# Splitting the causal mask of the scores between VectorE and ScalarE, with the places of the work set anew

## The chip, the core and the metric

The kernel runs on one core of one Trainium2 chip. The core has five engines that each work through an instruction queue of their own, in order: TensorE (matmuls), VectorE, ScalarE, GpSimd and SyncE, which here only issues DMAs. They meet at semaphores. The metric is the time of one execution on the device in microseconds (us), the median of several runs.

## What is computed

One transformer layer in fp32 for 8 sequences of 256 tokens, width 256: a layer norm, then an attention and a feed-forward part (FFN) that both read the normed input and are both added to the input.

```python
xn = layernorm(x)                                   # [8, 256, 256]
# attention, 16 heads of 128, 64 memory slots
q, k = rope(xn @ Wq.T), rope(xn @ Wk.T);  v = xn @ Wv.T;  g = xn @ Wg.T
s   = clip(xn @ Ws1.T @ Ws2.T + bs2, -32, 32)       # [b, h, t, 64]
es, enz = exp(s), exp(-cumlogsumexp(s, over tokens))
A   = where(causal, q @ k.T / sqrt(128), 0)         # scores, 256 x 256 a head and sequence
ok  = enz * (A @ es)                                # logits over the 64 slots
qv  = softmax(ok)
o   = where(causal, (qv * enz) @ es.T, 0) @ v
x1  = (rmsnorm(o) * w * silu(g)) @ Wo.T
# FFN, 2048 wide, weights as 4-bit codes with a scale for each 32
x2  = (gelu(xn @ Wg4.T) * (xn @ Wu4.T)) @ Wd4.T
out = x + x1 + x2
```

The line that matters here is `A`. The mask is causal: of a 256 x 256 block of scores, cut into four squares of 128, one lies wholly in the forbidden half and is never computed, two lie on the diagonal and need the triangle, and one, between queries 128 to 255 and keys 0 to 127, is wholly allowed.

## The kernel before

**Tiling.** The 2048 tokens are 4 groups of 512 (two sequences each). The attention works in 32 steps n: group g = n // 8 and a pair of heads. In each step, for the two heads j = 0, 1: `rope` (line 632) makes q and k on TensorE and turns them on ScalarE (copies of the two halves into z), VectorE (times the cosine) and GpSimd (times the sine, and the sum); `states` (575) makes es and enz; `value` and `gate` (669, 682) make v and the gate; `scores` (720), `logits` (735), `softmax` (771), `cross` (811), `weights` (835), `outputs` (879) and `close` (929) do the rest. Five kinds of data that need their rows and columns exchanged go out to DRAM and back (`scattered`, `turned`).

**The scores.** For a head j and each of the two sequences b, two matmuls fill 384 columns of one PSUM bank (of 8): keys 0 to 127 against all 256 queries (columns 0 to 255), keys 128 to 255 against queries 128 to 255 (columns 256 to 383). So the first and the third square of 128 lie on the diagonal, the second is the free one. `masked` then makes `at` in SBUF: one VectorE multiply of 384 columns with a mask whose squares are triangle, ones, triangle (`mask`, of which `tri` is the first square). `logits` multiplies `at` with es on TensorE, so it must wait for the four `at` of its step.

**The order.** The order of instructions on every engine is fixed when the program is built, by a planner written into the kernel. It holds a clock for each engine. A piece of work that follows a matmul is a generator (a "chain") whose `yield` gives the engine and a cost: `V(n)` is VectorE with 0.15 + 0.00105 n, `S(n)` ScalarE with 0.15 + 0.00088 n. `advance` always emits the instruction that could begin first; at equal times a chain of rank 0 (the masks are such) goes first. The matmuls of a step are placed by the tables: `POS` gives each unit's place in a step as a share of it, `START` other places for the steps -1 and 0 (-1 is what runs ahead of step 0), `NORM_AT` those of the later groups' norms, and `DUE` says how many pieces of FFN weights are to be decoded by each step. The FFN is cut into units (gate, up, down) that `feed` lays evenly between; `FIRST` and `LAST` weigh how many of them the first and last steps get. A unit whose operands would by the planner's clock come later than 0.3 (`SOON`) after TensorE's is put off: an FFN unit goes first, up to 4 ahead (`AHEAD`). The 8 PSUM banks go round in order, so a matmul that opens a bank waits until the reader of the bank 8 back is done.

The scores were made and masked like this:

Of the kernel before, what the change touches and what calls it, by code (L numbers as in the profile page):

```python
# [13 lines left out]
ALU = mybir.AluOpType  # L14
# [3 lines left out]
P = 128  # L18
# [14 lines left out]
WARM = 15  # L33


POS = {'scores': (0.054, 0.064),
 'logits': (0.12,),
 'softmax': (0.335,),
 'cross': (0.147,),
 'weights': (0.169,),  # L40
 'low': (0.121,),
 'states': (0.167,),
 'outputs': (0.364, 0.453),
 'close': (0.384, 0.559),
 'rope': (0.176, 0.315, 0.368, 0.485),
 'vg': (0.561, 0.79, 0.922, 0.953)}
START = {-1: {'states': (0.575,), 'rope': (0.155, 0.358, 0.421, 0.588)},
 0: {'vg': (0, 0.013, 0.059, 0.197),
     'scores': (0.082, 0.162),
     'states': (0.336,),  # L50
     'logits': (0.251,),
     'softmax': (0.433,),
     'rope': (0.211, 0.24, 0.245, 0.458)}}
FEED = {-1: (0.336, 1.0)}
NORMS = {0: 1, 2: 2, 5: 3}
WO = (1, 3, 4, 6)
NORM_AT = (0.204, 0.657)
FIRST = [0.27, 1.57]
LAST = [1.65, 3.53]
DUE = [4, 6, 7, 7, 9, 9, 10, 11, 11, 11, 12, 13, 14, 15, 16, 16, 16, 17, 18, 19, 19, 22, 23, 23, 24]  # L60


@with_exitstack
def layer_kernel(ctx: ExitStack, tc: tile.TileContext, a: dict, out: bass.AP):
# [15 lines left out]
    nc = tc.nc  # L80
# [21 lines left out]
    def V(n):  # L102
        return "v", 0.15 + 0.00105 * n

    def S(n):
        return "s", 0.15 + 0.00088 * n
# [97 lines left out]
    def bank():  # L204
        while not freed:
            advance()
        clock["pe"] = max(clock["pe"], freed.pop(0))
        t = ps_p.tile([P, 512], F32, tag="ps", name="ps", bufs=8)
        at_tag[id(t)] = t, []
        banks_taken.add(id(t))  # L210
        return t
# [6 lines left out]
    mask = const.tile([P, 3 * P], F32, tag="mask", name="mask")  # L218
    tri, ones = mask[:, 0:P], mask[:, P : 2 * P]
# [278 lines left out]
    def ffn():  # L498

        for q in range(4):  # L500
            for g in range(NG):
                for n in blocks(q):
                    yield ffn_gate, g, n
                    yield ffn_up, g, n
                for i in (0, 2):
                    yield ffn_down, g, q, i
# [204 lines left out]
        return pst, ps  # L711

    def masked(ts, pss):
        for t, ps in zip(ts, pss):
            yield V(384)
            nc.vector.tensor_tensor(t, ps[:, 0 : 3 * P], mask, ALU.mult)

    def scores(n, j):

        (q, qc), (k, kc) = of[n]["q", j], of[n]["k", j]  # L720
        need(qc, kc)
        pss, ats = [], []
        for b in range(2):
            ps = bank()
            nc.tensor.matmul(  # L725
                ps[:, 0:T], lhsT=k[:, b, 0:P], rhs=q[:, b, :], start=True, stop=True
            )
            nc.tensor.matmul(  # L728
                ps[:, T : T + P], lhsT=k[:, b, P:T], rhs=q[:, b, P:T], start=True, stop=True
            )  # L730
            pss.append(ps)
            ats.append(new(p2, [P, 3 * P], "at", 4))
        pe(1.3)
        of[n]["at", j] = ats, chain(masked(ats, pss), *ats, *pss, rank=0)
# [236 lines left out]
    banks = NG * (MLP // P * 2 + 8)  # L971
    weight = FIRST + [1.0] * (N + 2 - len(FIRST) - len(LAST)) + LAST
    feeding = list(ffn())
# [18 lines left out]
    ps = bank()  # L992
# [10 lines left out]
    for n in range(-1, N + 1):  # L1003
        at = []
        pos = START.get(n, {})

        def put(name, k, f, *args):
            place = pos.get(name, POS[name])
            at.append((place[k], len(at), f, args))

        def put_at(place, f, *args):
            at.append((place, len(at), f, args))

        def put_norm(g, places):
            for k, h in enumerate((0, 2)):
                put_at(places[k], norm, g, h)
# [24 lines left out]
        if gn:  # L1041
            if gn > 1:
                put_at(0.0, load_x, gn * TC, TC)
            put_norm(gn, NORM_AT)
        if n > 0:
# [14 lines left out]
        fed = upto  # L1060
        upto = DUE[n + 1] if n + 1 < len(DUE) else 24
        for k in range(sent, upto):
# [93 lines left out]
```

## Time and profile before

| | |
|---|---|
| median of 3 runs | 1188.27 us (1187.34 to 1188.94) |
| the profiled execution | 1187.13 us, of which the profile's span is 1185.3 us |
| instructions | 18158 |
| granted TensorE clock | 1.00 in every stretch |
| DMA | 135.30 MB, mean 114 GB/s, 38.5% of the 16 engines' time |
| HBM | read 88.47 MB, written 45.61 MB |

How the busy time lies over the span (us of busy time in each stretch; the stretches are in us from the span's start):

| stretch | TensorE | VectorE | ScalarE | GpSimd |
|---|---|---|---|---|
| 0 to 66 | 58.87 | 54.60 | 27.91 | 29.61 |
| 66 to 130 | 62.39 | 55.11 | 33.90 | 33.48 |
| 130 to 330 | 199.67 | 155.49 | 96.01 | 90.76 |
| 330 to 530 | 200.00 | 152.04 | 91.85 | 83.78 |
| 530 to 730 | 199.60 | 148.41 | 89.06 | 82.67 |
| 730 to 930 | 199.48 | 153.94 | 96.06 | 87.62 |
| 930 to 1130 | 200.00 | 139.90 | 89.80 | 79.12 |
| 1130 to 1185.3 | 51.89 | 25.20 | 11.68 | 7.07 |

In the profile a row of a group of instructions has the line of the kernel, the engine, the operation, the tiles written and read, partitions x elements, the number of instructions, then busy time in us, the mean of one in ns, and the engine's idle time just before with what ended it. TensorE's fp32 matmuls appear as two records each. A row of the timeline has start and duration in us, and in brackets an idle time before it and its releaser. Durations of neighbours overlap a little[...]. TensorE's ends are modelled, so that its busy time is not its peak rate; its waits are what can be read from it.

### The profile page before, as it was taken

The page shows a single profiled execution, that of the slowest core. Times are in us where ns is not written, and L with a number is a line of the kernel's source. Part 1 is how long each engine was busy: PE and PEld are TensorE (multiplying, and loading weights), DVE is VectorE, ACT ScalarE, POOL GpSimd, SP SyncE. Part 2 cuts the span into 40 slices and gives each one's busy share as a digit, 9 for nine tenths or more (in the row PEclk, how much of TensorE's full clock was granted, in tenths as well). Part 3 has the DMA queues.
Part 4 walks back from the last instruction along what each step waited for, and adds up shares of the span by engine and source line. Part 5 has one row for each costly group of instructions (what it writes and reads, how often), then busy time and mean ns, then how long its engine had stood idle before and what let it go on. Part 6 is the DMA issues. An engine that isn't in the chain of part 4 may idle for free.

```text
span 1185.3 us, 18158 instructions
## 1 busy us (share of the span) xinstructions
PE 1171.9 (99%) x5830; PEld 827.7 (70%) x5830; DVE 884.7 (75%) x1690; ACT 536.3 (45%) x1685; POOL 494.1 (42%) x439
## 2 busy tenths in 40 slices
PE   9899999999999999999999999999999999999998
PEld 6466776866767777667767677686776777766775
DVE  7978968887677788767587875968778577768553
ACT  3545535455344444443354543435544444445321
POOL 5434525554344444434344442434544334445110
PEclk9999999999999999999999999999999999999999
DMA  6335444453333342333344243434333333432321
GB/s 209 116 105 153 143 118 152 132 144 116 101 119 117 110 140 84 107 113 107 90 142 123 86 121 107 120 103 122 96 97 96 116 116 107 124 102 88 98 64 61
DMA packets 143087, 135.30 MB, mean 114 GB/s; under 512 B 21264, under 2 KB 110480, under 8 KB 142992
## 3 DMA queue, kind: packets, MB, share of 16 engines
q1 hardware_dynamic: 142992, 134.15, 38.5%
q8 instruction: 46, 0.75, 0.3%
q14 instruction: 49, 0.40, 0.1%
HBM read 88.47 MB, written 45.61 MB: 113 GB/s over the span
## 4 chain that ended last, share of the span: by engine, by line
PE 89%; DVE 6%; DMA 2%; issue 1%; POOL 1%; ACT 1%; SPq 1%; DVEq 0%; ACTq 0%; POOLq 0%
PE ps L645 17%; PE ps L706 17%; PE ps L491 9%; PE ps L941 9%; PE ps L437 8%; PE ps L466 8%; PE ps L888 5%; PE ps L725 4%; PE ps L745 3%; PE ps L845 3%; PE ps L728 2%; PE ps L584 2%; PE ps L872 1%; PE ps L820 1%; DVE enz L630 1%
## 5 line engine op out<-in xcount | busy, mean ns | idle before, releaser
L663 POOL TENSOR_TENSOR z<-z,turns 128x512 f32<-128x512 f32 x128 | 169.4, 1324 | 209.3 <-ACT z L656 209.0
L645 PE MATMUL ps<-xT,wts 128*128 128x512 f32 x512 | 239.2, 599 | 0.5 <-ACT xT L349 0.5
L706 PE MATMUL ps<-wts,xT 128*128 128x256 f32 x1024 | 235.7, 379 | 1.5 <-DVE og L914 1.1
L706 PEld LDWEIGHTS ps<-wts,xT 128*128 128x128 f32 x1024 | 194.4, 190 | 54.1 <-issue 24.4
L645 PEld LDWEIGHTS ps<-xT,wts 128*128 128x128 f32 x512 | 90.1, 190 | 82.0 <-issue 75.1
L446 POOL TENSOR_SCALAR t<-t 128x512 f32<-128x512 f32 x64 | 40.2, 629 | 196.6 <-ACT t L444 194.6
L437 PE MATMUL ps<-xT,w_gate 128*128 128x512 f32 x256 | 120.7, 594 | 0.1
L466 PE MATMUL ps<-xT,w_up 128*128 128x512 f32 x256 | 120.6, 594 | 0.0
L630 DVE RECIPROCAL enz<-enz 128x128 f32<-128x128 f32 x128 | 117.6, 932 | 0.0
L491 PE MATMUL ps<-w_down,inter 128*128 128x256 f32 x512 | 115.3, 380 | 0.0
L941 PE MATMUL ps<-w_o,ogT 128*128 128x256 f32 x496 | 112.1, 379 | 0.0
L941 PEld LDWEIGHTS ps<-w_o,ogT 128*128 128x128 f32 x496 | 94.1, 190 | 24.7 <-issue 12.4
L491 PEld LDWEIGHTS ps<-w_down,inter 128*128 128x128 f32 x512 | 96.6, 190 | 15.9 <-issue 3.2
L655 ACT COPY z<-ps 64x512 f32<-64x512 f32 x128 | 74.5, 582 | 69.8 <-PE ps L645 60.3
L444 ACT ACTIVATE t<-ps 128x512 f32<-128x512 f32 x64 | 38.2, 596 | 137.9 <-PE ps L437 137.8
L910 POOL TENSOR_TENSOR ss<-ss,nhalf 128x4 f32<-128x4 f32 x64 | 66.0, 1032 | 69.7 <-DVE ss L906 68.4
L409 DVE TENSOR_TENSOR res<-ps,res 128x512 f32<-128x512 f32 x63 | 42.9, 681 | 69.5 <-PE ps L491 48.0
L664 POOL TENSOR_TENSOR k<-k,z 128x512 f32<-128x512 f32 x64 | 83.7, 1308 | 26.5 <-DVE k L658 16.7
L664 POOL TENSOR_TENSOR q<-q,z 128x512 f32<-128x512 f32 x64 | 85.0, 1328 | 21.2 <-DVE q L658 17.2
L803 POOL TENSOR_TENSOR prT<-okT,enz 128x512 f32<-128x512 f32 x32 | 40.8, 1274 | 119.9 <-DMA okT<-by_way 106.6
L792 ACT ACTIVATE ok<-okT,mx 128x64 f32<-128x64 f32 x256 | 85.7, 339 | 10.8 <-DVE mx L786 10.3
L448 DVE TENSOR_TENSOR t<-ps,t 128x512 f32<-128x512 f32 x64 | 43.7, 684 | 60.9 <-POOL t L446 60.7
(83 smaller groups left out, 1936.6 us busy)
## 6 DMA issues: line engine op xcount, KB each, us to landing
wts<-in_wqkvg_dram SPq DMA_DIRECT2D x64, 512.0 KB, 3.8
by_way<-ok SPq DMA_DIRECT2D x256, 64.0 KB, 1.8
okT<-by_way SPq DMA_DIRECT2D x64, 256.0 KB, 2.7
by_way<-og SPq DMA_DIRECT2D x256, 64.0 KB, 1.8
ogT<-by_way SPq DMA_DIRECT2D x64, 256.0 KB, 2.9
by_way<-u SPq DMA_DIRECT2D x128, 64.0 KB, 1.8
u<-by_way SPq DMA_DIRECT2D x32, 256.0 KB, 2.8
pk<-in_codes_dram SPq DMA_DIRECT2D x12, 256.0 KB, 3.1
```

The lines of the kernel that those rows point to most:

```text
L437: nc.tensor.matmul(pg, lhsT=w_gate[:, c, ns], rhs=xT[:, c, gs], start=c == 0, stop=c == 1)
L466: nc.tensor.matmul(pu, lhsT=w_up[:, c, ns], rhs=xT[:, c, gs], start=c == 0, stop=c == 1)
L491: nc.tensor.matmul(ps[:, k, :], lhsT=inter[g, n][0][:, (i + k) * P : (i + k + 1) * P], rhs=w_dn[:, n, :], start=n == 2 * q, stop=n == 2 * ...
L630: nc.vector.reciprocal(r, r)
L645: nc.tensor.matmul(ps, lhsT=w[:, c, :], rhs=xT[:, c, g * G : (g + 1) * G], start=c == 0, stop=c == 1)
L655: nc.scalar.copy(z[0:64], pv[64:128])
L663: nc.gpsimd.tensor_tensor(z, z, sin_b, ALU.mult)
L664: nc.gpsimd.tensor_tensor(y, y, z, ALU.add)
L706: nc.tensor.matmul(ps[:, k, :], lhsT=xT[:, c, tt], rhs=w[:, which, c, :], start=c == 0, stop=c == 1,)
L792: nc.scalar.activation(pr[:, js, i, :], okT[:, js, i, :], AF.Exp, bias=mx[:, k : k + 1], scale=SCALE, accum_out=sm[:, k : k + 1],)
L910: nc.gpsimd.tensor_tensor(ss, ss, nhalf, ALU.pow)
L941: nc.tensor.matmul(ps[:, k, :], lhsT=ogT[hh][0][:, i + k], rhs=w_o[:, (hp // 2) * 4 + hh, :], start=hh == 0, stop=hh == 3,)
```

## The change

`masked` is rewritten. For each `at`, VectorE multiplies only the first and the third square (one instruction over 2 x 128 columns with a step between them, against the triangle used twice), and ScalarE copies the second square. Both write the same `at` tile and read the same PSUM bank. The rest of the code is as it was, with the third square of `mask` still made at the start. The tables have new numbers: the scores' place goes from 0.054 and 0.064 to 0, the logits' from 0.12 to 0.148, the softmax's, outputs', close's and low rank's are moved, so are places of the steps -1 and 0 and of the norm, the FFN's weights in the first and last steps, and four entries of `DUE`. With them the planner orders the instructions of all engines anew from the first step on; lines behind `masked` have numbers larger by 7 in the changed kernel (the multiply is L718, the copy L723).

```diff
-POS = {'scores': (0.054, 0.064),
- 'logits': (0.12,),
- 'softmax': (0.335,),
+POS = {'scores': (0, 0),
+ 'logits': (0.148,),
+ 'softmax': (0.404,),
  'cross': (0.147,),
  'weights': (0.169,),
- 'low': (0.121,),
+ 'low': (0.14,),
  'states': (0.167,),
- 'outputs': (0.364, 0.453),
- 'close': (0.384, 0.559),
+ 'outputs': (0.315, 0.453),
+ 'close': (0.367, 0.534),
...
-START = {-1: {'states': (0.575,), 'rope': (0.155, 0.358, 0.421, 0.588)},
- 0: {'vg': (0, 0.013, 0.059, 0.197),
-     'scores': (0.082, 0.162),
+START = {-1: {'states': (0.727,), 'rope': (0.155, 0.358, 0.421, 0.588)},
+ 0: {'vg': (0.044, 0.057, 0.103, 0.241),
+     'scores': (0.068, 0.162),
...
-     'softmax': (0.433,),
-     'rope': (0.211, 0.24, 0.245, 0.458)}}
+     'softmax': (0.411,),
+     'rope': (0.238, 0.267, 0.272, 0.485)}}
...
-NORM_AT = (0.204, 0.657)
-FIRST = [0.27, 1.57]
-LAST = [1.65, 3.53]
-DUE = [4, 6, 7, 7, 9, 9, 10, 11, 11, 11, 12, 13, 14, 15, 16, 16, 16, 17, 18, 19, 19, 22, 23, 23, 24]
+NORM_AT = (0.204, 0.593)
+FIRST = [0.1, 1.57]
+LAST = [1.56, 3.5]
+DUE = [4, 6, 7, 7, 8, 9, 10, 11, 11, 11, 12, 13, 14, 15, 15, 16, 16, 16, 18, 19, 19, 22, 22, 23, 24]
...
     def masked(ts, pss):
+
+        tri_b = tri.unsqueeze(1).to_broadcast([P, 2, P])
         for t, ps in zip(ts, pss):
-            yield V(384)
-            nc.vector.tensor_tensor(t, ps[:, 0 : 3 * P], mask, ALU.mult)
+            yield V(256)
+            nc.vector.tensor_tensor(
+                t.rearrange("p (k q) -> p k q", q=P)[:, ::2],
+                ps[:, 0 : 3 * P].rearrange("p (k q) -> p k q", q=P)[:, ::2], tri_b, ALU.mult,
+            )
+            yield S(128)
+            nc.scalar.copy(t[:, P : 2 * P], ps[:, P : 2 * P])
```

## The prediction

> **What bounds the kernel now.** I read the page's first part, then TensorE's waits, then the rows of the changed operation, then the timeline around it. First part (busy us, share of the span, instructions):
>
> ```profile
> PE 1171.9 (99%) x5830; PEld 827.7 (70%) x5830; DVE 884.7 (75%) x1690; ACT 536.3 (45%) x1685; POOL 494.1 (42%) x439
> ```
>
> TensorE is busy for 1171.9 of 1185.3 us, at a granted clock of 1.00 in every stretch. VectorE, which the change relieves, is busy for three quarters. All that a change beside TensorE can win is in TensorE's waits (total us, times, longest):
>
> ```profile
> PE ps L725 <- POOL k L664: 3.0, 2, 2.6
> PE ps L745 <- DVE at L716: 1.7, 3, 1.3
> PE ps L706 <- DVE og L914: 1.1, 1, 1.1
> ...
> PE ps L706 <- DVE inter L475: 0.5, 1, 0.5
> ...
> PE ps L725 <- DVE t L452: 0.4, 1, 0.4
> PE ps L745 <- DVE off L306: 0.4, 1, 0.4
> PE ps L888 <- DVE wt L855: 0.3, 1, 0.3
> ```
>
> The rest of the 13.4 us: 2.0 us before and around the first matmuls, about 3.1 us after the last one, and gaps too small for a name, the same in both kernels. What can change is 7.0 us. By the timeline, step by step: n=0 0.40+0.48, n=1 2.61+1.34+0.19, n=3 1.06+0.40, later 0.18+0.38. (The 0.33 at 1145.7 us stays: the last 19 groups of TensorE's program are the same.) Even all of it would be 0.6%. The line that the change rewrites, with its neighbours by size, from the groups with shapes kept apart (busy us, mean ns | idle before):
>
> ```profile
> L716 DVE TENSOR_TENSOR at<-ps,mask 128x384 f32<-128x384 f32 x128 | 64.1, 545 | 0.6 <-PE ps L728 0.5
> L855 DVE TENSOR_TENSOR wt<-ps,mask 128x512 f32<-128x512 f32 x64 | 40.7, 676 | 2.5 <-PE ps L845 2.5
> L598 DVE TENSOR_SCALAR esT<-ps 128x256 f32<-128x256 f32 x64 | 24.0, 416 | 19.5 <-PE ps L845 18.7
> L829 ACT COPY cross<-ps 128x256 f32<-128x256 f32 x32 | 11.9, 373 | 68.4 <-PE ps L820 68.3
> ```
>
> Only 1.7 us of TensorE's waits is put down to those 64.1 us of VectorE, in three places. A usual step shows why (start, duration; TensorE, then VectorE):
>
> ```profile
> 932.51 0.38 PE L728 MATMUL ps<-q,k 128*128 128x128 f32 x2
> 932.73 1.88 PE L437 MATMUL ps<-xT,w_gate 128*128 128x512 f32 x4
> 934.45 1.88 PE L466 MATMUL ps<-xT,w_up 128*128 128x512 f32 x4
> 936.26 1.52 PE L745 MATMUL ps<-at,es 128*64 128x256 f32 x16
> ```
> ```profile
> 931.55 1.94 DVE L716 TENSOR_TENSOR at<-ps,mask 128x384 f32<-128x384 f32 x4
> ```
>
> The scores end at 932.9, the four masks at 933.5, and the logits start at 936.26 behind two FFN units: 2.8 us to spare.
>
> **The change, part by part.**
>
> *The split.* Removed: 128 multiplies of 384 elements, 545 ns each. Added: 128 multiplies of 2x128 and 128 copies of 128. From 545 and 676 ns the slope is 1.02 ns an element, so 256 elements are about 0.41 us (L598, another operation of that size, has 416 ns); the copy, from 373 ns at 256 and 580 at 512 (L679), about 0.27 us. VectorE loses 128 x 0.13 = 17 us, ScalarE gains 128 x 0.27 = 35 us (45% to 48% busy). Neither bounds the end: directly nothing for TensorE.
>
> *The new wait.* In the built program every copy waits for VectorE, and the logits then wait for ScalarE. So the two parts of one mask are in series: 0.41 + 0.27, plus about 0.05 us of handover (VectorE to ScalarE 0.03 to 0.05 in the timeline), 0.74 us against 0.545. **Here a rule speaks against the change**: the Trainium skill, "PSUM — Partial Sum Buffer", section "Terms", says that two engines may not read one bank in the same partitions at once. By the row alone, with the copy beside the multiply, a mask would be ready 0.13 us sooner; by the rule it is 0.2 us later. No run here shows such a double read; the built program's waits side with the rule, and I take 0.2 us later. A second rule, "Perfetto Trace Analysis", section "Optimizing Scalar/DVE Operations", has each instruction pay a fixed access cost (about 125 ns for VectorE on PSUM, 51 for ScalarE) and advises grouping. By rows the fixed part of VectorE is 545 - 384 x 1.02 = 153 ns. If the split's extra engine time (0.41 + 0.27 - 0.545 = 0.14 us, 128 times) were on TensorE's path, the sum would be +18 us; by the waits only the steps without cover pay.
>
> Behind a waiting copy on ScalarE stand the tanh of the FFN gate, the copies of the next cross state and the rope's halves, on which TensorE waits through banks and operands. In the usual step they come after all four copies or are done before.
>
> *The places.* TensorE's program has the same matmuls in another order. Between the second head's scores and the logits stood 1.7 to 8.6 us of other work, mostly FFN, in 28 steps and nothing in 4 (n = 1, 3, 6, 15). Now it is the cross matmul (0.54 us) and mostly one FFN unit: at least 2.3 us in 29 steps, and 0.54 us in n = 1, 3, 31. Cover of 2.3 us against a last mask that needs 0.74 after its matmul, for a logits half that starts 0.65 us later still: 2.2 us spare, against at most one instruction ahead on each queue (0.93 VectorE, 0.60 ScalarE). Hidden. Changes of array shape cost 0.10 us each (two L491 units take 6.9 us, and 7.01 when the next is L745); there are 118, before 116: **+0.2**. DMAs: same transfers, each issued with the work that feeds it; the order on SP changes by a place or two (a turn of ok or og before or after a weight load). At 38.5% DMA share I cost that at nothing; where a turn slips behind a 512 KB load (3.8 us to landing) it hits the early steps, below.
>
> *Step 0*: now scores come before most of the value and gate work, 5 us sooner, and only 5.2 us of other work stands before the logits (8.6 before). VectorE's queue of decoding is what is late, because it stalls beside GpSimd:
>
> ```profile
> 21.69 1.42 DVE L392 TENSOR_SCALAR u<-u 128x512 int32<-128x512 int32 x1
> ```
> ```profile
> 21.18 1.65 POOL L664 TENSOR_TENSOR q<-q,z 128x512 f32<-128x512 f32 x1
> ```
>
> L392 takes 0.42 us elsewhere (36.04 us); here it ends 0.28 us after GpSimd's L664. Walking the new order with these durations: the bank of the last rope comes free at about 25.1 us, wanted at 24.4 (0.7; without the stalls 0; I take 0.35). The third and fourth mask stand behind 2 scans, 3 reciprocals, 2 FFN steps and a norm's statistics (1.27 us), and are whole at 34.0 and 35.7; the logits' halves want them at 33.3 and 34.65: 0.7 + 1.05. **2.1** (0 to 2.5), before 0.88.
>
> *Step 1*: the 2.61 us was the last rope of the step: its product came from GpSimd at 55.95, its scores were due at 53.4. Now an FFN unit (1.72) stands between the two heads' scores; the same chain (z buffer, ScalarE, two GpSimd passes of 1.27) behind a softmax pass of 1.3 us on ScalarE comes at about 55.2, due at 54.0: 1.2. Then the logits: the fourth copy stands behind the cross copy (0.37) and a tanh (0.63): 0.8. **2.0** (0.4 to 4.1), before 4.14.
>
> *Step 3*: two norm passes (1.15) and the cross copy stand before the third copy: 0.95; of the bank wait (1.06, before) I keep half: **1.45** (0.4 to 2.5), before 1.46. *Later*: in step 31 the cross copy is ahead of the last two mask copies with 0.54 us of cover: 0.6; other small waits 0.5: **1.1**, before 0.56.
>
> Sum: 2.1 + 2.0 + 1.45 + 1.1 + 0.2 = 6.85 against 7.04: -0.2 us. From the profiled execution (1185.3 us span, 1.83 around it, 1187.13) that is 1186.9; the median of the three runs shown is 1.1 above that execution, so **1188.1**.
>
> **Rivals.**
> - *The early steps run clear.* For: the split takes 0.13 us from VectorE per mask just where its queue is the late one (83% busy in the first 66 us), and the new order puts cover at both of step 1's waits. Against: step 0 loses 3.4 us of cover. Step 0 0.7, step 1 0.8, step 3 0.6, later 0.5, shapes 0.2: 2.8 us, so 1188.27 - 4.24 = 1184.0.
> - *The copies wait in every step.* Place: ScalarE's queue before the logits. With two instructions of each engine ahead of the last mask (2 x 0.68 + 2 x 0.60 + 0.74 = 3.3 us) the cover of 2.3 + 0.65 falls short by about 0.3 us; in 23 steps that is +7, 1195. It decides from 2.2 us of queue on. For: L745 waits for two engines in turn, with less cover than before. Against: in the usual step both queues stand empty there (VectorE waits 1.0 us just before 930.95).
> - *The early steps get worse*, by banks held until the copy: +4, 1192.
> - *The split does nothing that TensorE sees*: this is the first case, since only the order then counts.
>
> **How the numbers follow.** A measurement of this kernel tells about 0.2% (2.4 us) from no change. Near the old time (own range 1185.9 to 1190.6): 0.47. Early steps clear: 0.30. Copies wait everywhere 0.12, early steps worse 0.11. So faster 0.30, same 0.47, slower 0.23. The range takes in the clear case and half of the slower ones: 1183.8 to 1191.6.
>
> **What would show it.** L718 near 0.41 us and L723 near 0.27; VectorE about 17 us less, ScalarE 35 more; TensorE's busy time the same within 1 us, its waits still nearly all before 130 us, now put down to ScalarE's at in L752. Wrong if L752 waits for at in more than some five steps, or if L732's wait for k and the first logits' wait are both gone.

## The result and the profile after

The changed kernel takes 1190.72 us (median of 9 runs, 1190.15 to 1191.87) against 1187.69 for the kernel before: 1.0024 of it, 95% interval 1.0015 to 1.0032. It is slower by 3.0 us: inside the range of the forecast, but the other way from its likeliest case, a gain of 0.2 us.

First part of the page of the changed kernel (busy us, share of the span, instructions):

```profile
PE 1174.8 (99%) x5830; PEld 830.0 (70%) x5830; DVE 877.2 (74%) x1690; ACT 569.2 (48%) x1813; POOL 491.2 (41%) x439
```

The span is 1188.4 us, 3.1 more. TensorE has the same 5830 records and is "busy" 2.9 us longer: not all of the loss is waiting. The rows of the split, from the groups with shapes kept apart (busy us, mean ns | idle before):

```profile
L718 DVE TENSOR_TENSOR at<-ps,mask 128x256 f32<-128x256 f32 x128 | 50.2, 415 | 4.4 <-PE ps L735 3.9
L723 ACT COPY at<-ps 128x128 f32<-128x128 f32 x128 | 33.8, 265 | 54.1 <-DVE at L718 49.1
```

The two take 415 and 265 ns, as worked out; the copies' idle time is put down to their own multiplies. TensorE's waits (total us, times, longest):

```profile
PE ps L852 <- POOL prT L810: 4.6, 3, 3.7
PE ps L732 <- POOL k L664: 2.0, 1, 2.0
PE ps L752 <- ACT at L723: 1.1, 3, 0.7
PE ps L1001 <- DVE mask L262: 1.0, 1, 1.0
PE ps L437 <- DVE sgate L694: 0.5, 1, 0.5
```

A line stands on top that the kernel before did not have: the `weights` matmuls (L852) wait for prT, the softmax of the step before, once for 3.7 us. The logits wait for ScalarE's `at` for 1.1 us in all, in three places. The timeline of TensorE there (start, duration, and idle time before with its releaser):

```profile
61.65 0.70 PE L584 MATMUL ps<-rT,w_s 64*128 64x256 f32 x4
66.07 1.66 PE L852 MATMUL ps<-prT,esT 64*128 64x128 f32 x16 [3.72 <-POOL prT L810]
67.51 1.07 PE L879 MATMUL ps<-cross,prT 64*128 64x128 f32 x8
```

The kernel before, same place (there `weights` is L845):

```profile
61.79 3.72 PE L491 MATMUL ps<-w_down,inter 128*128 128x256 f32 x16
65.44 0.70 PE L584 MATMUL ps<-rT,w_s 64*128 64x256 f32 x4
66.07 3.72 PE L491 MATMUL ps<-w_down,inter 128*128 128x256 f32 x16
69.72 0.49 PE L845 MATMUL ps<-prT,esT 64*128 64x128 f32 x4
```

prT is not late by itself. GpSimd makes it once a step; the first of the 32 starts at 64.8 us in the changed kernel and at 67.2 before (shortest, median and longest in ns, then the first and last start):

```profile
L810 POOL TENSOR_TENSOR prT<-okT,enz x32: 1261/1271/1278, 64.8 to 1139.4; 128x512 f32<-128x512 f32 x32
L803 POOL TENSOR_TENSOR prT<-okT,enz x32: 1262/1270/1386, 67.2 to 1135.5; 128x512 f32<-128x512 f32 x32
```

But two down units, 6.9 us, stood around the states and ahead of the weights, and in the new order they stand behind the weights, so TensorE arrives at 62.3.

The other part of the loss is in how long the same matmuls take: L852's sixteen records took 1.06 us in a usual step and 1.66 here. The busy time by stretch (length, then busy us of PE, PEld, DVE, ACT and POOL; granted TensorE clock; DMA share; GB/s) of the changed kernel:

```profile
56.00:60.00 4.00, 4.00 (x20) 3.33 (x22) 4.00 (x9) 2.33 (x7) 0.62 (x1) 0.57 0.28 75
```
```profile
66.00:70.00 4.00, 3.93 (x26) 3.06 (x27) 2.20 (x5) 1.26 (x2) 0.02 (x1) 0.57 0.02 5
```

and of the kernel before, which waits 2.61 us just ahead:

```profile
57.00:60.00 3.00, 1.66 (x13) 0.99 (x12) 2.96 (x8) 0.97 (x2) 0.00 (x0) 1.00 0.35 94
```

Asked in stretches of half a microsecond, the clock of the changed kernel is 0.50 from about 56.3 to 59.7 and from about 66.6 to 70.0 us: twice 3.4 us, each right behind a wait (1.97 us for k, 3.72 for prT). At half clock a busy TensorE loses 1.7 us in such a period.

So the first theory, the **order theory**, says that the new places put TensorE idle twice in step 1, and that each time half clock follows. Its rival, the **split theory**, says that the masks are whole later and the logits pay.

### The profile page after: what moved, and what is told of

It reads as the page before. It is cut to its first block, busy times and chain, and to the rows that moved or that the text cites. A ratio compares the mean times of both kernels' runs of the same rounds, so it can differ in the third digit from the quotient of the medians.

```text
span 1188.4 us, 18234 instructions
## 1 busy us (share of the span) xinstructions
PE 1174.8 (99%) x5830; PEld 830.0 (70%) x5830; DVE 877.2 (74%) x1690; ACT 569.2 (48%) x1813; POOL 491.2 (41%) x439
## 4 chain that ended last, share of the span: by engine, by line
PE 89%; DVE 6%; DMA 2%; SPq 1%; issue 1%; ACT 1%; POOL 0%; DVEq 0%; POOLq 0%
PE ps L706 17%; PE ps L645 17%; PE ps L948 9%; PE ps L491 9%; PE ps L437 8%; PE ps L466 8%; PE ps L895 5%; PE ps L732 4%; PE ps L752 3%; PE ps L852 3%; PE ps L735 2%; PE ps L584 1%; PE ps L827 1%; PE ps L879 1%; DVE enz L630 1%
## 5 line engine op out<-in xcount | busy, mean ns | idle before, releaser
L692 ACT ACTIVATE sgate<-ps 128x512 f32<-128x512 f32 x64 | 37.9, 598 | 103.3 <-PE ps L706 97.5
L895 PEld LDWEIGHTS ps<-v,wt 128*128 128x128 f32 x512 | 67.0, 191 | 28.9 <-issue 23.0
```

The costliest lines, as they stand in the source:

```text
L895: nc.tensor.matmul(po[:, i, :], lhsT=wt[:, i, :], rhs=v[:, i, j * DK : (j + 1) * DK], start=False, stop=i == TC - 1,)
```

## Experiments

Each was timed over several rounds beside the kernel before on the same chip, which took 1187.97 us beside the first four, 1188.08 beside the next and 1187.45 beside the last. So compare the ratios, which are to it; that of the changed kernel is the 1.0024 above, as it was not timed again. The clock is the granted one, a mean over each run: one period of 3.4 us at half clock brings it to 0.9986 (shown as 0.999), two bring it to 0.997.

| kernel | median us | ratio, 95% interval | mean clock over its runs |
|---|---|---|---|
| split, before's tables | 1190.78 | 1.0022 (1.0014 to 1.003) | 0.997 to 1.000 |
| places, old masks | 1190.21 | 1.0016 (1.0009 to 1.0022) | 0.994 to 0.997 |
| changed, both waits filled | 1187.51 | 0.9992 (0.9986 to 0.9999) | 1.000 |
| changed, weights at 0.32 | 1192.34 | 1.0035 (1.0023 to 1.0048) | 0.996 to 1.000 |
| split, order of before | 1187.11 | 0.9992 (0.9984 to 1.0) | 0.997 to 1.000 |
| before, its wait filled | 1187.82 | 0.9997 (0.9988 to 1.0005) | 1.000 |
| changed, step 1 laid out anew, a | 1197.04 | 1.008 (1.0067 to 1.0093) | 0.996 |
| changed, step 1 laid out anew, b | 1188.94 | 1.0008 (0.9999 to 1.0016) | 0.997 to 1.000 |
| split, order of the places | 1189.59 | 1.0018 (1.0011 to 1.0025) | 0.994 to 0.997 |
| changed, one rope first | 1186.67 | 0.9995 (0.9987 to 1.0004) | 0.997 to 1.000 |
| the same, both waits filled | 1186.05 | 0.9986 (0.998 to 0.9993) | 1.000 |
| split, order of before, filled | 1186.42 | 0.9991 (0.9983 to 0.9999) | 0.999 to 1.000 |

### The split and the places, each alone

The kernel before with the new `masked`; and the changed kernel with the old one.

> The kernel before with the new masked alone, all tables as before. The order theory (the 3 us of the changed kernel come from two idle stretches of TensorE in step 1 that the new places make, 1.97 us ahead of the second head's scores and 3.72 us ahead of the weights of step 0, and from the two periods of 3.4 us at half clock that follow them): no 3.7 us wait ahead of L852, since two down units stand before it as before; time 1187.7 +- 1.5, granted clock 0.999 to 1.000. The split theory (each mask is whole 0.2 us later because the copy waits for VectorE, and the logits pay): 2 to 4 us slower than before, with waits of L752 for ScalarE's at in more than five steps.

> The changed kernel with the old masked (one VectorE multiply of 384), all tables as changed. The order theory: TensorE has the weights of step 0 straight behind the states again, so it waits 3 to 4 us for prT there, clock 0.996 to 0.998, time 1190.7 +- 1.5. The split theory: back to the time before, 1187.7, clock 1.000.

Neither theory had both runs right. The places alone are slow as expected, with a wait of 4.47 us for prT and 3.50 for k in the profile and clocks down to 0.994. But the split with before's tables is as slow, 1190.78, with nearly full clock. Its TensorE waits:

```profile
PE ps L732 <- POOL k L664: 4.3, 2, 2.7
PE ps L752 <- ACT at L723: 2.1, 3, 1.3
...
PE ps L437 <- ACT at L723: 0.9, 1, 0.9
PE ps L437 <- PE ps L584: 0.6, 1, 0.6
```

There is no wait for prT, but a new one of 1.6 us for k (in step 3), a bank held until its copy was done (0.9 us), and the logits' waits, in three places only. In all the waits that can change are 9.3 us, against 7.0 before: 2.3 more, which is most of the 2.8 us, with no half clock in the profile. Either these are the split's own, or they come from the planner, which had laid everything in another order once it was told of the new costs.

### The split in an unchanged order

```diff
-            yield V(256)
+            yield V(384)
             nc.vector.tensor_tensor(...)
-            yield S(128)
             nc.scalar.copy(t[:, P : 2 * P], ps[:, P : 2 * P])
```

The planner is left at the old cost, so that all engines keep the old order, and the copies are put in behind their multiplies. Once with before's tables, once with the changed ones.

> The kernel before with the split masks, but with the planner left at the old cost of one VectorE step (384) for both, so that every engine has its instructions in the order of before and the 128 copies are put in behind their multiplies. The split alone with before's places was 2.8 us slower, with a full clock in most runs; there the planner had reordered everything. If that loss is the split's own (a mask whole 0.2 us later, a copy that holds ScalarE's queue): 1190 to 1191 again, with waits of L751 for ScalarE's at. If it is the planner's other order that costs (its places no longer fit): 1188.0 +- 0.7.

> The changed kernel's places with the split masks, but the planner left at the old cost of one VectorE step of 384, so that the order is that of the places alone (1190.2, with waits of 3.5 us for k and 4.5 us for prT in its profile) with the copies put in. With before's places the split in an unchanged order won 1 us. If the split as such is harmless or a small gain, and the places are the loss: 1189 to 1190.5, clock still 0.994 to 0.998, the wait for prT still above 3 us. If the split costs where the cover before the logits is short: slower than the places alone by 1 us or more, with L751 or L752 waiting for ScalarE's at for over 1.5 us in all.

With before's order (in the traces TensorE, VectorE and GpSimd have every instruction in its old place) the split is harmless: 1187.11, 0.9992 (0.9984 to 1.0), at least no loss. TensorE's timeline shows what became of the waits of step 1 (before: 2.61, then 1.34 and 0.19):

```profile
55.32 0.70 PE L731 MATMUL ps<-q,k 128*128 128x256 f32 x2 [1.91 <-POOL k L664]
59.20 2.40 PE L751 MATMUL ps<-at,es 128*64 128x256 f32 x12 [1.19 <-ACT at L722]
```

VectorE, shorter by 0.13 us a mask, brings k 0.7 us sooner, and the later masks don't cost what that wins. (In this execution the scores ran at half clock, which covers a part of the masks; with that wait filled, below, and full clock, the logits wait 1.65 us, 0.1 more than before.) With the places' order it is the same: 1189.59 beside 1190.21 for the places alone (1.0018 and 1.0016, no difference). So **the 3 us are the order's, not the split's**: each of the new orders, from new costs, from new tables or from both, cost 2 to 3 us.

### The clock

Products of ones go into the bank that the waiting matmuls are to fill, just ahead of them. TensorE is busy in place of idle, and nothing comes sooner.

```diff
+        for _ in range(15 if n == 0 else 0):     # weights; 8 in scores, where (n, j, b) == (1, 1, 0)
+            nc.tensor.matmul(pss[0][:, 0:P], lhsT=ones, rhs=ones, start=True, stop=True)
         for i in range(TC):
```

> The changed kernel with 8 products of ones ahead of the second head's scores of step 1 and 15 ahead of the weights of step 0, each into a bank that the real products overwrite: TensorE is kept busy (about 1.8 and 3.3 us) while it would wait, and the waits are left as they are. If the half clock follows from those idle stretches: clock 1.000, the bursts at half speed gone, and 3.4 us won, 1187.3 +- 0.7. If the lower clock has another cause (more work in all, the phase of a run): clock still 0.997 and 1190.7.

> The kernel before with 10 products of ones (2.2 us) ahead of the second head's scores of step 1, where TensorE waits 2.6 us. In 21 of its 51 runs the kernel before had a mean clock of 0.997, in 17 of 0.999. If its own wait in step 1 makes those: clock 1.000 in all runs, and the median falls by about 0.5 us, to 1187.4. If not: clocks spread as before, 1188.0.

The changed kernel has a clock of 1.000 in 21 of 21 runs, where it had 0.996 or 0.997 in 9 of 9, and takes 1187.51 us: 3.2 us less by the medians, 3.8 by the ratios. The fillers (`ps<-mask`, the ones), the real work behind them, and the stretch with the weights of step 0 (as in the tables above, clock 1.00):

```profile
55.17 2.05 PE L733 MATMUL ps<-mask 128*128 128x128 f32 x16 [0.29 <-DVE k L658]
62.55 3.62 PE L851 MATMUL ps<-mask 128*128 128x128 f32 x30
66.37 1.16 PE L856 MATMUL ps<-prT,esT 64*128 64x128 f32 x16 [0.21 <-POOL prT L812]
66.00:130.00 64.00, 63.79 (x312) 44.07 (x310) 50.69 (x108) 35.63 (x113) 31.67 (x29) 1.00 0.48 141
```

TensorE's real work waits as long as before, and all engines have their other instructions in the same order. The half clock is therefore caused by the idle stretches, and **with the stretches filled the whole loss is gone**. Not all of that can be read as clock. In the two profiled executions, 2.5 us apart, the filled one gains 2.2 us between the first scores of step 1 (50.78 and 51.62 us) and the first unit behind the weights (71.05 and 69.73), less than the 3.4 of two periods, since a part of the first passes under the wait for prT. It gains about 1.1 in two later waits that it does not have (0.50 us for prT at 552 us, 0.54 for `sgate` at 757), and it had lost 0.8 in step 0 to a wait for k that the other does not have; why these differ is open.

The kernel before had its periods too: of the 33 runs beside its filled variant, 23 had less than 1.000, and filled it has 1.000 in 13 of 13. But there they cost little: 1187.82 filled, 0.9997 with 1 inside the interval, so the expected half microsecond is not shown. Its runs with 0.997 were on average 1.2 to 1.4 us longer than those with 1.000, on each of the three chips. Its profiled run happened to have none.

### Giving the weights of step 0 work ahead

The tables take an entry for a single step, here for step 1 (the table's a and b are the second and third line).

```diff
-START = {-1: {...
+START = {1: {'weights': (0.32,), 'outputs': (0.4, 0.5)}, -1: {...                                     # weights at 0.32
+START = {1: {'weights': (0.34,), 'outputs': (0.5, 0.6), 'scores': (0, 0.17), 'logits': (0.18,)}, ...  # a
+START = {1: {'weights': (0.34,), 'outputs': (0.5, 0.6), 'scores': (0, 0.13), 'logits': (0.2,)}, ...   # b
+START = {1: {'weights': (0.25,), 'outputs': (0.33, 0.453)}, ...                                       # one rope first
```

> The changed kernel with one entry more in START: in step 1 the weights of step 0 stand at 0.32 and its outputs at 0.4 and 0.5, so that two ropes and a down unit (6.9 us) come before them. Order theory: the wait of 3.72 us for prT is gone and one of the two periods at half clock with it (clock about 0.9985); 3.7 + 1.7 us won, 1185.3 +- 1. Rival (the prT wait only hides one that is behind it, such as the wait for wt or for banks): a wait of 2 us or more turns up before 100 us, and less than 2 us are won.

> The changed kernel with places of their own for step 1: second head's scores at 0.17 and logits at 0.18, weights at 0.34, outputs at 0.5 and 0.6, so that the cross matmul and the states stand ahead of the second scores, a down unit and a rope ahead of the weights, and two ropes ahead of the outputs. Order theory: the waits of 1.97 and 3.72 us are gone and no other of more than 1.2 us takes their place, clock 0.999 or above: 5.7 + 3.2 us less, about 1183.5 (1182.5 to 1185.5), faster than both kernels. Rival (the later stages of step 1 are late in any case, as where only the weights were moved): a wait of 2 us or more for wt, prT or k before 140 us, and 1187 or more.

> As the last one, but the second head's scores stay where they were (behind one up unit), and the logits go behind the cross matmul, the states and a rope. The wait of 1.97 us for k stays, the one for prT goes: clock 0.998 to 1.000, about 1186 (1184.5 to 1187.5). Rival as there.

All three missed what the order theory expected. With 6.9 us of work ahead the wait for prT is gone, and the rival holds: 1192.34. VectorE shows it (weights at 0.32; start, duration, idle before):

```profile
70.83 0.76 DVE L598 TENSOR_SCALAR esT<-ps 128x256 f32<-128x256 f32 x2 [5.44 <-PE ps L852]
...
76.30 1.26 DVE L862 TENSOR_TENSOR wt<-ps,mask 128x512 f32<-128x512 f32 x2
```

and TensorE behind it:

```profile
77.01 1.25 PE L895 MATMUL ps<-v,wt 128*128 128x128 f32 x8 [3.08 <-DVE wt L862]
```

L598 clips the states of step 2 into `esT`, a tile of two buffers, and the weights of step 0 read the buffer it is to overwrite. VectorE's queue stands still until L852 is done, and all that is behind it, the masks of the weights among it, is late. In `a` this wait is 7.75 us, and TensorE waits 3.57 us for wt and 2.30 for the next prT; `b` waits 0.96 and 2.49. That the buffer is the cause is read from the code and these rows; a third buffer was not tried. It would explain why later is worse: the weights must neither come before prT nor long after.

> The changed kernel with the weights of step 0 at 0.25 in step 1 and its first outputs at 0.33: one rope (1.72 us) comes before the weights, the down unit stays behind them. The wait for prT is read as 2.0 us in place of 3.72 and nothing behind it gets later than before: 1.7 us less for the wait, and up to 1.7 more where one period at half clock falls away, 1187.3 to 1189. If the work behind is late in any case (as where the weights were moved further): a wait for wt of over 1 us, and 1190 or more.

> The last one with 8 products of ones ahead of the second scores of step 1 and 6 ahead of the weights of step 0. Clock 1.000 in all runs; against the changed kernel with both waits filled (1187.5) the shorter wait for prT, 1.7 us: 1185.8 +- 0.8, faster than both kernels.

One rope ahead of the weights is the middle: 1186.67, a little better than expected. Its timeline has the wait as read, and nothing behind it came later:

```profile
65.51 1.16 PE L852 MATMUL ps<-prT,esT 64*128 64x128 f32 x16 [2.02 <-POOL prT L810]
```

With both waits filled it takes 1186.05, 0.9986 (0.998 to 0.9993): **faster than both kernels**, by 0.14% and 0.38% on their ratios.

> The split in the unchanged order of before (1187.1) with 8 products of ones ahead of the second scores of step 1. Its runs had clocks of 0.997 to 1.000; with the wait filled 1.000 in all, and 0.3 to 1 us less: 1186.5, faster than both kernels by more than their intervals.

It takes 1186.42, as expected. The split in the old order is worth about as much, once its idle stretch is filled; both gains are about 0.1%, with intervals that end just below 1.

## Why the prediction was wrong

*The split*: right. 415 and 265 ns for 0.41 and 0.27; ScalarE 33 us more for 35. VectorE fell by 7.5 us, not 17. Its split rows fell by 13.9 (busy time counts the overlap of neighbours once, 128 x 0.13 counts it twice), and decoding took 5.5 us more in the new order: an L388 takes 662 ns where a GpSimd operation runs beside it and 277 where none does, and 32 of the 48 do so now, 19 before. That the split costs TensorE nothing by itself was said, and the run in the unchanged order shows it. The rule that two engines may not read a bank at once (the Trainium skill, "PSUM — Partial Sum Buffer", "Terms") agrees with what was built, copies behind multiplies; no run here shows both reading at once. Its price of 0.2 us a mask was without effect.

*The places, in the usual step*: right. From 132 to 1105 us the changed kernel has two waits, 0.50 and 0.54 us, and the logits wait for `at` nowhere.

*Step 0*: 2.1 us forecast, 0.72 found. The bank wait did not come: the multiply of k ended at 25.2, as walked, but the group that I had waiting for it started at 24.7, so it opened another bank than I had counted.

*Step 1*: **here it failed first.** I walked k (1.2 forecast, 1.97 found) and the masks (0.8 forecast, none found, since TensorE at half clock came later), and wrote "**2.0** (0.4 to 4.1)". The step found is 5.69. The term left out is prT: TensorE's new order had L584 and then L852, with the down units moved behind, and I weighed only what stands ahead of the logits. I had the number at hand: GpSimd's first L803 stands at 67.2 us in the trace of before, behind 6.9 us of down units. Every matmul that lost cover in the new order had to be asked for its operand, not only the one that the change names.

*The sum*: **it priced a wait at its length, and here it failed again.** The waits that can change come to 8.23 us, where the forecast has 6.65 (6.85 less 0.2 for the array shapes): 1.2 more than before. That is less than half of the 3.0 us. The rest is two periods at half clock, for which the sum has no term. In the profile of before the clock was 1.00 throughout, with a wait of 2.61 us in it, so I took the clock for settled. Of the two periods 2.2 us can be read in the profiles; with the 1.2 of waits that is 3.4, for 3.0 measured, and the difference is open. A part of the waits for masks hides under the half clock (0.47 us come back when it is filled).

*Steps 3 and later*: 1.45 forecast, 0.21 found (no bank wait); 1.1 forecast, 1.61 found, 0.86 of it once more for prT (0.50 in step 15, 0.36 in step 31).

*The rivals and the range*: that 1190.7 lies in the range is luck. The range took in half of the two slower cases, and both named the wrong cause. The copies' wait in every step was not found; a bank held until the copy cost 0.9 us in one place of the split with before's tables, and nothing in the changed kernel. The fast case, with step 1 at 0.8, has 5.69 against it. Of the signs named, TensorE's busy time "the same within 1 us" failed (2.9 more, by the half clock), and most of the waits stand under prT and not under ScalarE's at.

## What to carry to other kernels

When an order is changed, list for every matmul that lost work ahead of it when its operand is ready, not only for the one whose operand was changed; in a kernel at 99% of TensorE, one uncovered operand in the first steps outweighs a whole engine's relief. Price an idle stretch of TensorE of about 2 us or more at its length and, behind it, one or two periods at half clock of up to 1.7 us each, less what passes under the next wait; and look at the clock of several runs, since one profile can miss it. Before a stage is moved later for cover, ask which buffer it still reads: the next writer's engine stops in its queue.

## What the runs showed of the hardware

A wait of 1.97 us was enough for half clock in the changed kernel's profile, while 2.61 us in that of before was not; over 51 runs, the kernel before had 0.997 in 21 and 1.000 in 9. The half-clock periods measure 3.41 us, or twice that (56.74 to 63.57 us in the split in the unchanged order), and within a run they begin whole multiples of it apart: at 56.33 and 66.57 us in the changed kernel (three), at 57.47 and 77.95 with the weights at 0.32 (six). The Trainium skill, "TensorE: Matmul & The Clock Gate", section "Part 1: The HAM clock gate (the "warmup" mystery)", gives a free-running window of 3413 ns, which agrees.

A wait counts by how it falls into such a window. Each trace's record of the granted clock begins at a border of this grid (at 5.13 us in the changed kernel, 15 windows ahead of 56.33), so TensorE's idle time (with its modelled ends) can be added up by window in all 14 profiles, up to its last matmul. Of 12 windows at full clock with 1.9 us or more, 11 were followed by half clock (the exception is the kernel before, with 1.98); of the others, all with 1.71 or less, none was. A half-clock window was followed by another one in the 3 cases with 0.7 us or more of idle time in it, and in none of the 11 with 0.25 or less. The 1.97 us of the changed kernel lay wholly in one window. With one rope first, the same wait was as long, but a border of the grid at 54.69 us cut it into 0.83 and 1.16, and the clock stayed full:

```profile
55.84 0.70 PE L732 MATMUL ps<-q,k 128*128 128x256 f32 x2 [1.98 <-POOL k L664]
```

In its section "Why this matters for your kernels" the same page asks for no idle gap of more than about 3 us; here 1.97 was already too long, and the measurement decides. With the waits filled by products that nobody reads, the clock stayed at 1.000 in 21 of 21, 13 of 13 and 21 of 21 runs of three kernels, and in 12 of 13 of a fourth.
